# An RWKV block on one core: last tile's output stored in three parts from two queues, flag of inexact weights formed four steps sooner

## Chip, cores and metric

The kernel runs on one core of one Trainium2 chip. The metric is the device time of one execution in microseconds (us); the number to predict is the median of unprofiled runs. The engines are named as the profile names them: PE is TensorE's matmuls and PEld its weight loads, DVE is VectorE, ACT is ScalarE, POOL is GpSimd and SP is SyncE.

## The reference

Input `x` is (2, 4096, 256) in float32. An RWKV layer with a layer norm ahead of it, then a gated feed-forward layer with a layer norm ahead of it:

```python
x = x + attn(layernorm(x))      # W_k, W_v, W_r, a scan over time, W_o
x = x + ffn(layernorm(x))

def ffn(x):                     # D_IN 256, D_HID 1024; w1, w2, h1, h2, w3 hold -1, 0 or 1
    h = silu(tlin(x, w1_w, w1_s)) * tlin(x, w2_w, w2_s)
    h = gelu(tlin(h, h1_w, h1_s))
    h = gelu(tlin(h, h2_w, h2_s))
    return tlin(h, w3_w, w3_s)
```

`tlin(x, w, s)` is `x @ w.T * s`.

## The kernel before

Features lie on the 128 partitions and time on the free axis. Time is cut into 16 tiles of 512 steps (2 batches of 8). A tile of `x` is `[128, 2, 512]` float32, 512 KB: two halves of the 256 features, numbered h=0 and h=1. The result is summed into the same tile, `x_sb` (called `x1` in `ffn`), and stored from it.

`split_block` does the work. Its feed-forward weights are held rounded to a format in which the matmul takes one pass (float32r), and each activation is split into a rounded part `hi` and a rest `lo`, so that every product takes two matmuls, L172 for `hi` and L173 for `lo`. This gives the wanted result only if the rounding left the weights unchanged. So the kernel compares the given weights with the rounded ones while it runs (`compare`, on tiles 1 to 15), and sums the counts of differences at the end: `total` on DVE (L629), the matmul `everywhere` with a constant matrix, which brings the sum to all partitions (L631), and `inexact`, an integer 0 or 1, on DVE (L633). Every engine then reads `inexact` into a register (L60) and branches (L61): if it is 1, `general_block` computes everything again in plain float32. With the weights of the reference it is 0, and all engines branch over that block. The closing barrier of the program carries the line of the launch, L908.

For tile i, `ffn(i)` is a generator that yields 26 times. Steps 0 to 7 make the gated products (`pa`, `pb`); steps 8 to 15 are the first hidden layer and steps 16 to 23 the second, both with eight groups of 16 matmuls into `ph`, each followed by two ACT instructions (L580, L582) and a DVE subtraction that makes `lo` (L583). The second layer's weights come from HBM in eight blocks, `h2_sb`, that SP loads (L576). Steps 24 and 25 are the output product for h=0 and h=1: 16 matmuls into `po`, and one DVE instruction that adds the result to `x_sb` (L595). After that POOL issues one DMA for the tile (L599). Between the steps the loop takes steps of the next tiles' attention and layer norm, but there are none left during the last tile.

The order on each engine is that of a scheduler that works by priority of the program's order, unless an `issue_after` ties an instruction down. In the program before, the order at the end is: on PE the last `po` group, then `everywhere`, then the register load; on DVE the two L595, then `inexact`; on SP the last `h2_sb` load, then the register load; on POOL the last store, then the register load. `total` is placed far earlier, at 1431.7 us.

Of the kernel before, what the change touches and what calls it, by code (L numbers as in the profile page):

```python
# [8 lines left out]
F32 = mybir.dt.float32  # L9
F32R = mybir.dt.float32r  # L10
AF = mybir.ActivationFunctionType
ALU = mybir.AluOpType

P = 128
# [3 lines left out]
NH = HID // P  # L18
# [47 lines left out]
def split_block(ctx, tc, flags, x, vecs, w_attn, w1, w2, h1, h2, w3, out):  # L66


    nc = tc.nc
    tensor, vector, scalar = nc.tensor, nc.vector, nc.scalar  # L70
# [9 lines left out]
    ps_attn = ctx.enter_context(tc.tile_pool(name="ps_attn", bufs=3, space=bass.MemoryType.PSUM))  # L80
# [3 lines left out]
    tiles = [(b, n) for b in range(B) for n in range(NT)]  # L84

    def hbm(t, b, n):
        return t[b, :, n * TS : (n + 1) * TS].rearrange("(h p) t -> p h t", p=P)

    whole = slice(0, TS)
    halves = [slice(k * TS // 2, (k + 1) * TS // 2) for k in range(2)]  # L90
# [11 lines left out]
    for m, queue in enumerate((nc.scalar, nc.sync, nc.sync)):  # L102
# [6 lines left out]
        out=ident, in_=ident, compare_op=ALU.not_equal, fill=1.0, base=0, pattern=[[-1, P]], channel_multiplier=1  # L109
# [16 lines left out]
    mean_w = const.tile([P, P], F32, name="mean_w")  # L126
# [15 lines left out]
    pieces = []  # L142
# [4 lines left out]
    rounded = const.tile([P, len(pieces) + NH * (NH * P // PIECE)], F32, name="rounded")  # L147
    found = iter(range(rounded.shape[1]))

    def compare(kept, given, shape):  # L150
        raw = tmp.tile(shape, F32, tag="full", name="raw")
        nc.gpsimd.dma_start(out=raw, in_=given)
        j = next(found)
        vector.scalar_tensor_tensor(
            raw, raw, 1.0, kept.bitcast(F32), ALU.mult, ALU.not_equal, accum_out=rounded[:, j : j + 1]
        )

    def col(base, j):
        return vec[:, base + j : base + j + 1]
# [7 lines left out]
    def split_product(psum, weights, src):  # L167

        n = len(src)
        for c in range(n):  # L170
            hi, lo = src[c]
            tensor.matmul(psum, weights(c), hi, start=c == 0, stop=False)  # L172
            tensor.matmul(psum, weights(c), lo, start=False, stop=c == n - 1)  # L173
# [3 lines left out]
    def split(hi, lo, full):  # L177

        marks["rounded"] = scalar.activation(hi, full, AF.Copy)  # L179
        marks["rest"] = vector.tensor_tensor(lo, full, hi.bitcast(F32), ALU.subtract)  # L180
# [92 lines left out]
    def normalise(i):  # L273

        x_sb = loaded.pop(i)
        if i + 1 < len(tiles):
            loaded[i + 1] = load_x(i + 1)
        xn = []

        def new_xn():  # L280

            xn.append(one.tile([P, ND, TS + 1], F32, tag="xn", name="xn"))
            if tiles[i][1] == 0:
                vector.memset(xn[0][:, :, 0:1], 0.0)
            else:
                vector.tensor_copy(xn[0][:, :, 0:1], prev)
            return xn[0][:, :, 1:]

        yield from layernorm(x_sb, new_xn, "rstd1", pause=i == 1)
        vector.tensor_copy(prev, xn[0][:, :, TS:])  # L290
        normal[i] = (x_sb, xn[0])
# [107 lines left out]
    def first_tile(second):  # L399
# [59 lines left out]
        attn, ffn = (ps_attn, "pa"), (ps_ffn, "pf")  # L459
        keys = [[(project(0, 0, attn, p), p) for p in halves], [(project(0, 1, attn), whole)]]  # L460
        v = [project(1, h, ffn) for h in range(ND)]
        r = [project(2, h, ffn) for h in range(ND)]

        def differences(h):
# [47 lines left out]
        for p in halves:  # L512
            add(y[:, 1, p], so[1][0][:, p], r[1][:, p], ALU.mult)
        banks = [
            [pool.tile([P, TS // 2], F32, tag=tag, name="ps_o") for pool, tag in kinds]
            for kinds in ((attn, attn), (attn, ffn))
        ]
        for c in range(ND):
# [28 lines left out]
    def hidden():  # L547
        return (
            hid.tile([P, TS], F32R, tag="hi", name="hi"),
            hid.tile([P, TS], F32R, tag="lo", name="lo"),  # L550
        )

    def ffn(i, x1, x2):

        checks = pieces[2 * (i - 1) : 2 * i] if i > 0 else []
        ha = []
        for f in range(NH):
            fs = slice(f * P, (f + 1) * P)
            pa = ps_ffn.tile([P, TS], F32, tag="pf", name="pa")
            split_product(pa, lambda c: w1_sb[:, c, fs], x2)  # L560
            pb = ps_ffn.tile([P, TS], F32, tag="pf", name="pb")
            split_product(pb, lambda c: w2_sb[:, c, fs], x2)
            full = tmp.tile([P, TS], F32, tag="full", name="gated")
            scalar.activation(full, pa, AF.Silu, scale=col(S1, f))  # L564
            vector.scalar_tensor_tensor(full, pb, col(S2, f), full, ALU.mult, ALU.mult)  # L565
            hi, lo = hidden()
            split(hi, lo, full)
            ha.append((hi, lo))
            yield
        for layer, scales in enumerate((SH1, SH2)):  # L570
            src, ha = ha, []
            for f in range(NH):
                fs = slice(f * P, (f + 1) * P)
                if layer == 1:
                    block = stream.tile([P, NH, P], F32R, tag="h2", name="h2_sb")
                    nc.sync.dma_start(out=block.bitcast(F32), in_=h2_hbm[f].bitcast(F32))  # L576
                ps = ps_ffn.tile([P, TS], F32, tag="pf", name="ph")
                split_product(ps, lambda c: block[:, c, :] if layer else h1_sb[:, c, fs], src)
                hi, lo = hidden()
                scalar.activation(hi, ps, AF.Gelu, scale=col(scales, f))  # L580
                full = tmp.tile([P, TS], F32, tag="full", name="full")
                scalar.activation(full, ps, AF.Gelu, scale=col(scales, f))  # L582
                vector.tensor_tensor(lo, full, hi.bitcast(F32), ALU.subtract)  # L583
                ha.append((hi, lo))
                if layer == 0 and f % 4 == 0 and checks:
                    compare(*checks.pop(), [P, PIECE])
                if layer == 1 and i == f + 1:
                    n = PIECE // P
                    for c in range(0, NH, n):
                        compare(block[:, c : c + n, :], h2[:, c : c + n, fs], [P, n, P])  # L590
                yield
        for h in range(ND):
            ps = ps_ffn.tile([P, TS], F32, tag="pf", name="po")
            split_product(ps, lambda c: w3_sb[:, c, h * P : (h + 1) * P], ha)
            vector.scalar_tensor_tensor(  # L595
                x1[:, h, :], ps, col(S3, h), x1[:, h, :], ALU.mult, ALU.add
            )
            yield
        nc.gpsimd.dma_start(out=hbm(out, *tiles[i]), in_=x1)  # L599

    def run(steps):
        for _ in steps:
            pass

    normal, got = {}, {}
    second = normalise(1)
    first_tile(second)
    for i in range(len(tiles)):
        ahead = attention(i + 1) if i + 1 < len(tiles) else iter(())
        further = normalise(i + 2) if i + 2 < len(tiles) else iter(())  # L610
        for step, _ in enumerate(ffn(i, *got.pop(i))):
            if i == 0:
                if step in (1, NH - 1):
                    with tc.issue_after(marks["rounded"].ins), tc.issue_after(marks["rest"].ins):
                        next(second)
                elif step == NH:
                    run(second)

            for _ in range(0 if step < NH else 4 if step == NH + (i == 0) else 1):
                next(ahead, None)  # L620
            if step > 2 * NH - 6 and step % 2 == 0:
                next(further, None)
        run(ahead)
        run(further)
    assert len(pieces) <= 2 * (len(tiles) - 1)


    total = flags.tile([P, 1], F32, name="total")
    vector.tensor_reduce(total, rounded, mybir.AxisListType.X, ALU.add)  # L629
    everywhere = ps_attn.tile([P, 1], F32, tag="pa", name="everywhere")  # L630
    tensor.matmul(everywhere, mean_w, total, start=True, stop=True)  # L631
    inexact = flags.tile([P, 1], mybir.dt.int32, name="inexact")
    vector.tensor_scalar(inexact, everywhere, 0.0, None, ALU.is_gt)  # L633
    return inexact[0:1, 0:1]


# [275 lines left out]
```

## Time and profile before

| | us |
|---|---|
| median of 3 runs without a profile | 1572.11 (1571.52 to 1572.32) |
| the profiled execution, whole | 1574.68 |
| its span, first to last instruction | 1572.90 |
| PE busy | 1559.1 |
| DVE busy | 1102.0 |
| ACT busy | 1034.4 |
| POOL busy | 62.0 |
| last matmul of the output product starts | 1562.62 |
| last addition to `x_sb` starts (0.75 long) | 1563.06 |
| last store issued | 1564.11 |

The span counts from the first instruction to the last; what lies around it belongs to the launch and is not resolved. The granted TensorE clock was 0.997 of full speed over the span. Durations of matmuls are modelled, so a busy PE is not PE at its peak. A page shows the instruction groups with the most busy time; the register loads, branches, semaphore waits and drains of the program's end don't count as busy and are found by asking for their source line.

### The profile page before, as it was taken

What the parts mean: (1) busy time and instruction counts of PE and PEld (TensorE: products, weight loads), DVE (VectorE), ACT (ScalarE), POOL (GpSimd) and SP (SyncE); (2) the same over time, 40 slices, a digit from 0 to 9 for tenths busy, and PEclk for the clock granted to TensorE, in tenths of its full rate; (3) what the DMA queues carried; (4) which work ended last, traced back from release to release, by engine and by line L of the source; (5) the groups of instructions that cost most, each with busy time, mean ns of one, the idle gap of its engine ahead of it and who ended that gap; (6) DMA issues with size and microseconds to landing.
All of it is one profiled execution on the core that took longest, in us unless ns stands there. A gap on an engine that the chain in (4) does not pass through costs nothing.

```text
span 1572.9 us, 16652 instructions
## 1 busy us (share of the span) xinstructions
PE 1559.1 (99%) x6319; PEld 1185.9 (75%) x6319; DVE 1102.0 (70%) x1763; ACT 1034.4 (66%) x1394; POOL 62.0 (4%) x99
## 2 busy tenths in 40 slices
PE   9999999999999999999999999999999999999997
PEld 5768777777777778777787777877777787777886
DVE  6788686776768767786786867767687676865521
ACT  5676767667577585776767666675776857756542
POOL 3000000000000000000000000000000000000000
PEclk9999999999999999999999999999999999999999
DMA  9102031220402204021130311203112030211202
GB/s 360 42 32 103 14 121 34 73 88 9 130 30 75 79 20 134 14 90 65 34 121 14 107 48 47 94 14 108 41 64 78 21 108 27 80 48 34 94 14 69
DMA packets 36598, 109.16 MB, mean 69 GB/s; under 512 B 3680, under 2 KB 12384, under 8 KB 36000
## 3 DMA queue, kind: packets, MB, share of 16 engines
q1 hardware_dynamic: 19136, 67.93, 13.0%
q0 software_dynamic: 16960, 39.59, 8.1%
q8 instruction: 51, 0.84, 0.2%
q10 hardware_dynamic: 416, 0.52, 0.1%
q14 instruction: 35, 0.29, 0.1%
HBM read 99.64 MB, written 12.58 MB: 71 GB/s over the span
## 4 chain that ended last, share of the span: by engine, by line
PE 80%; issue 15%; DVE 2%; ACT 1%; DMA 1%; POOL 0%; POOLq 0%; DVEq 0%
PE ph L172 24%; PE ph L173 24%; PE pb L172 3%; PE pa L172 3%; PE pb L173 3%; PE pa L173 3%; PE po L173 3%; PE po L172 3%; PE ps_k L165 3%; PE ps_r L165 3%; PE ps_v L165 3%; PE ps_o L165 3%; PE mean L201 1%; DVE scale L342 0%; PE var L201 0%
## 5 line engine op out<-in xcount | busy, mean ns | idle before, releaser
L172 PE MATMUL ph<-hi,h_sb 128*128 128x512 f32 x2048 | 813.8, 397 | 0.0
L173 PE MATMUL ph<-lo,h_sb 128*128 128x512 f32 x2048 | 801.4, 391 | 0.0
L172 PEld LDWEIGHTS ph<-hi,h_sb 128*128 128x128 f32 x2048 | 384.9, 188 | 92.7 <-issue 11.7
L173 PEld LDWEIGHTS ph<-lo,h_sb 128*128 128x128 f32 x2048 | 385.0, 188 | 88.6 <-issue 8.4
L583 DVE TENSOR_TENSOR lo<-full,hi 128x512 fp32r<-128x512 f32 x256 | 175.4, 686 | 174.7 <-ACT full L582 173.6
L580 ACT ACTIVATE hi<-ph,vec 128x512 fp32r<-128x512 f32 x256 | 175.7, 686 | 183.3 <-PE ph L173 181.9
L582 ACT ACTIVATE full<-ph,vec 128x512 f32<-128x512 f32 x256 | 174.2, 681 | 0.9 <-DVE lo L583 0.8
L565 DVE SCALAR_TENSOR_TENSOR gated<-pb,vec,gated 128x512 f32<-128x512 f32 x128 | 95.5, 748 | 58.2 <-PE pb L173 31.0
L580 ACT ACT_TABLE_LOAD x102 | 130.9, 1283 | 1.8
L564 ACT ACTIVATE gated<-pa,vec 128x512 f32<-128x512 f32 x128 | 86.5, 684 | 59.7 <-PE pa L173 56.5
L220 DVE RECIPROCAL rstd<-rstd 128x512 f32<-128x512 f32 x30 | 100.4, 3346 | 5.3 <-ACT rstd L218 5.3
L172 PE MATMUL pb<-x_hi,w_sb 128*128 128x512 f32 x256 | 102.1, 399 | 0.6 <-DVE gated L565 0.6
L172 PE MATMUL pa<-x_hi,w_sb 128*128 128x512 f32 x256 | 102.0, 398 | 0.1
L173 PE MATMUL pb<-x_lo,w_sb 128*128 128x512 f32 x256 | 100.7, 393 | 0.0
L173 PE MATMUL pa<-x_lo,w_sb 128*128 128x512 f32 x256 | 100.6, 393 | 0.0
L173 PE MATMUL po<-lo,w_sb 128*128 128x512 f32 x256 | 100.3, 392 | 0.0
L172 PE MATMUL po<-hi,w_sb 128*128 128x512 f32 x256 | 100.1, 392 | 0.0
L179 ACT ACTIVATE hi<-gated 128x512 fp32r<-128x512 f32 x128 | 80.6, 630 | 27.9 <-DVE gated L565 26.5
L180 DVE TENSOR_TENSOR lo<-gated,hi 128x512 fp32r<-128x512 f32 x128 | 87.7, 686 | 5.3 <-ACT hi L179 0.7
L248 DVE TENSOR_TENSOR_SCAN lm<-vec,lm,ps_k 128x512 f32<-128x512 f32 x30 | 38.3, 1278 | 42.9 <-PE ps_k L165 42.8
L303 DVE SCALAR_TENSOR_TENSOR mx<-xn,vec,mx 128x512 f32<-128x512 f32 x90 | 66.4, 744 | 0.3
L595 DVE SCALAR_TENSOR_TENSOR x_sb<-po,vec,x_sb 128x512 f32<-128x512 f32 x32 | 24.0, 751 | 58.9 <-PE po L173 58.9
(144 smaller groups left out, 1815.8 us busy)
## 6 DMA issues: line engine op xcount, KB each, us to landing
h_sb<-h_hbm SPq DMA_DIRECT2D x128, 512.0 KB, 3.3
out<-x_sb POOLq DMA_DIRECT2D x16, 512.0 KB, 3.1
raw<-in_h POOLq DMA_DIRECT2D x32, 256.0 KB, 3.1
x_sb<-in_x POOLq DMA_DIRECT2D x15, 512.0 KB, 4.1
h_sb<-in_h POOLq DMA_DIRECT2D x1, 4096.0 KB, 20.6
h_hbm<-in_h POOLq DMA_DIRECT2D x8, 512.0 KB, 22.9
w_sb<-in_w POOLq DMA_DIRECT2D x3, 1024.0 KB, 11.4
raw<-in_w POOLq DMA_DIRECT2D x12, 256.0 KB, 2.8
```

Source lines behind the costliest of these rows:

```text
L165: tensor.matmul(psum, weights(c), src[c], start=c == 0, stop=c == n - 1)
L172: tensor.matmul(psum, weights(c), hi, start=c == 0, stop=False)
L173: tensor.matmul(psum, weights(c), lo, start=False, stop=c == n - 1)
L179: marks["rounded"] = scalar.activation(hi, full, AF.Copy)
L180: marks["rest"] = vector.tensor_tensor(lo, full, hi.bitcast(F32), ALU.subtract)
L220: vector.reciprocal(rstd, rstd)
L303: vector.scalar_tensor_tensor(mx[:, h, :], xn[:, h, 1:], vec[:, j : j + 1], mx[:, h, :], ALU.mult, ALU.add)
L564: scalar.activation(full, pa, AF.Silu, scale=col(S1, f))
L565: vector.scalar_tensor_tensor(full, pb, col(S2, f), full, ALU.mult, ALU.mult)
L580: scalar.activation(hi, ps, AF.Gelu, scale=col(scales, f))
L582: scalar.activation(full, ps, AF.Gelu, scale=col(scales, f))
L583: vector.tensor_tensor(lo, full, hi.bitcast(F32), ALU.subtract)
```

## The change

In the last tile each half of the features is stored as soon as it is added. Half h=0 is one DMA of 256 KB from SP's queue. Half h=1 is two DMAs of 128 KB, its first 256 time steps from SP's queue and the other 256 from ACT's. POOL stores only the tiles 0 to 14, as before. The three operations that form the flag move into a function that is called after step 22 of the last tile, that is, ahead of the last `ph` group and of the output product; the assertion ahead of the loop is a check at build time.

```diff
@@ ffn @@
             vector.scalar_tensor_tensor(
                 x1[:, h, :], ps, col(S3, h), x1[:, h, :], ALU.mult, ALU.add
             )
-            yield
-        nc.gpsimd.dma_start(out=hbm(out, *tiles[i]), in_=x1)
+
+            if i == len(tiles) - 1:
+                for queue, p in ((nc.sync, halves[0]), (nc.scalar, halves[1])) if h else ((nc.sync, whole),):
+                    queue.dma_start(out=hbm(out, *tiles[i])[:, h, p], in_=x1[:, h, p])
+            yield
+        if i < len(tiles) - 1:
+            nc.gpsimd.dma_start(out=hbm(out, *tiles[i]), in_=x1)
@@ split_block @@
+    def any_inexact():
+
+        total = flags.tile([P, 1], F32, name="total")
+        vector.tensor_reduce(total, rounded, mybir.AxisListType.X, ALU.add)
+        everywhere = ps_attn.tile([P, 1], F32, tag="pa", name="everywhere")
+        tensor.matmul(everywhere, mean_w, total, start=True, stop=True)
+        inexact = flags.tile([P, 1], mybir.dt.int32, name="inexact")
+        vector.tensor_scalar(inexact, everywhere, 0.0, None, ALU.is_gt)
+        return inexact
+
+    assert len(pieces) <= 2 * (len(tiles) - 1)
...
             if step > 2 * NH - 6 and step % 2 == 0:
                 next(further, None)
+            if i == len(tiles) - 1 and step == 3 * NH - 2:
+                inexact = any_inexact()
         run(ahead)
         run(further)
-    assert len(pieces) <= 2 * (len(tiles) - 1)
-
-
-    total = flags.tile([P, 1], F32, name="total")
-    vector.tensor_reduce(total, rounded, mybir.AxisListType.X, ALU.add)
-    everywhere = ps_attn.tile([P, 1], F32, tag="pa", name="everywhere")
-    tensor.matmul(everywhere, mean_w, total, start=True, stop=True)
-    inexact = flags.tile([P, 1], mybir.dt.int32, name="inexact")
-    vector.tensor_scalar(inexact, everywhere, 0.0, None, ALU.is_gt)
     return inexact[0:1, 0:1]
```

The scheduled order of the changed program on the queues that it touches: on PE `everywhere` stands ahead of the last `ph` group. On DVE `inexact` stands behind the sixth `lo` of the second layer (1549.78 in the profile before) and ahead of the seventh (1553.40). On SP the register load stands behind the last `h2_sb` load, then come the two stores, then the branch. On ACT the store stands behind the last L582, then the register load, then the branch. On POOL the register load follows the store of tile 14.

## The prediction

> **What bounds the kernel now.** I read the busy times of the page first, then the timeline of the last tile, then the instruction groups by source line of the program's end, and the waits of SyncE's queue last.
>
> ```profile
> PE 1559.1 (99%) x6319; PEld 1185.9 (75%) x6319; DVE 1102.0 (70%) x1763; ACT 1034.4 (66%) x1394; POOL 62.0 (4%) x99
> ```
>
> TensorE is busy for 99% of the span, back to back, so nothing earlier is worth anything unless it shortens the matmul stream. The change doesn't: the number of matmuls stays, and one is only moved. What it can reach is the stretch in which TensorE has already stopped. The timeline of that stretch:
>
> ```profile
> 1562.62 0.40 PE L173 MATMUL po<-lo,w_sb 128*128 128x512 f32 x1
> ...
> 1562.86 0.28 PE L631 MATMUL everywhere<-total,mean_w 128*128 128x1 f32 x2
> 1563.06 0.75 DVE L595 SCALAR_TENSOR_TENSOR x_sb<-po,vec,x_sb 128x512 f32<-128x512 f32 x1 [2.91 <-PE po L173]
> 1563.73 0.15 DVE L633 TENSOR_SCALAR inexact<-everywhere 128x1 int32<-128x1 f32 x1
> 1564.11 0.73 POOL L599 DMA_DIRECT2D out<-x_sb  x1 [79.86 <-DVE inexact L633]
> ```
>
> The last useful matmul ends at 1563.02, the last output half is in SBUF at 1563.81, and the span ends at 1572.9. Nearly 10 us hold one 512 KB store and the program's end. POOL's row blames the flag (L633), but by the program's order its store waits for x_sb (L595, done 1563.81) and starts 0.30 later. The groups of L60 (every engine reads the flag into a register), L61 (every engine branches over the general block) and L908 (the closing barrier) show who comes last (durations are smallest/median/largest in ns, then the first and last start in us; a q after the engine's name is its queue):
>
> ```profile
> L60 ACTq TENSOR_LOAD <-inexact x1: 469/469/469, 1563.9 to 1563.9; - x1
> L60 DVEq TENSOR_LOAD <-inexact x1: 542/542/542, 1563.9 to 1563.9; - x1
> ...
> L61 ACTq COMPARE_BRANCH  x1: 50/50/50, 1564.4 to 1564.4; - x1
> L61 PEldq COMPARE_BRANCH  x1: 4422/4422/4422, 1564.5 to 1564.5; - x1
> ...
> L61 ACTq EVENT_SEMAPHORE  x1: 17/17/17, 1567.0 to 1567.0; - x1
> L61 DVEq EVENT_SEMAPHORE  x1: 21/21/21, 1567.7 to 1567.7; - x1
> L61 PEldq EVENT_SEMAPHORE  x1: 51/51/51, 1569.0 to 1569.0; - x1
> ...
> L908 POOLq DRAIN  x3: 51/113/7234, 1564.8 to 1572.6; - x3
> L908 SPq DRAIN  x3: 7/7/7, 1570.2 to 1572.3; - x3
> ```
>
> No engine may branch before the flag exists at 1563.9, and after the branch ACT needs 2.5 us to its next instruction (1564.44 to 1566.95), DVE 3.1 (1564.53 to 1567.68), PE 4.4; in that time the trace has fetches on the instruction queues. SyncE waits for the store before it joins the barrier:
>
> ```profile
> SPq L908 <- DMA out<-x_sb: 3.7, 1, 3.7
> DMA to landing us min/median/max: 3.0/3.1/5.5
> ```
>
> The second line is of the stores of L599: 3.1 us usually, 5.5 for this last one, whose final ring reports at 1569.64, 2.6 us after most of the others, while instruction fetches of 8 and 16 KB run. SyncE then works through ten more waits and arrives at 1570.27. The very last is POOL: its drain, begun at 1564.82 behind its store, lasts 7.23 us, to 1572.06. From there the barrier takes 0.84 to the end (1572.90). So the order of arrival is ACT 1567.0, DVE 1567.8, PE 1569.1, SP 1570.3, POOL 1572.1.
>
> **The change, part by part.** All sums are against the profiled execution: 1574.68 us, of which 1572.90 are span and 1.78 lie around it. The unprofiled median is 1572.11, 2.57 less; I carry a difference over to it unscaled.
>
> *The flag four steps sooner.* In the changed program's order the matmul `everywhere` stands ahead of the last `ph` group (about 1551.9), `inexact` between two `lo` subtractions; the reduction `total` stays where it ran (1431.7). The matmul has two passes. A row for its price: the 128x1 passes of the first tile (`var`, L342) start 0.11 apart. Two make 0.22 us that now stand inside the stream instead of after it; bounds 0.1 (one pass hidden) and 0.5 (two exposed weight loads of 0.19 and a refill). I take **+0.2**. On DVE `inexact` (0.15) runs at about 1552.5; behind it in the queue stands a `lo` that can't start before 1553.4, so it costs nothing as long as `everywhere` isn't late by 0.9.
>
> *Everybody's register load.* SP and POOL read the flag near 1552.5 and are through. On SP the load now stands before the two stores, behind the last `h2` load (1544.84), so nothing is held up. PE's queue runs ahead of its array: its wait for the last h2 block is recorded at 1548.14, the matmul that needs the block runs near 1551.9. The last `lo` that PE must wait for is ready at 1557.7, so its load and branch should be dispatched near 1560 and its 4.42 us of refill end by 1565, under the closing matmuls: PE's arrival falls from 1569.1 to about 1563.8.
>
> *The store.* POOL loses its last L599 store; with no transfer of its own since 1483.5 its drain should start near 1553, and even at 7.2 us it ends by 1561. SP gets h=0 (256 KB, issued near 1560.4, done by about 1563 under the last eight matmul pairs) and half of h=1; ACT gets the other half. h=1 is ready at 1563.81 + 0.2 = 1564.0. A steady SP issue lasts 0.32 and its first packet runs 0.95 after its start, against 0.73 and 1.31 for POOL's store; POOL's late start of 0.3 goes too (ACT and SP reacted to `inexact` within 0.04). 2 x 128 KB are half of a store of 3.1: I take 2.3 to landing, 1566.4; bounds 2.0 and 5.5 (this store's own row). Then SP's waits at 0.06 each: SP arrives at about **1567.1**.
>
> *What is late next.* ACT has its store ahead of its flag load: 1564.0 + 0.5 issue (its two DMAs at the start took 0.48 and 0.51) + 0.5 load + 0.1 branch + 2.5 refill = **1567.6**. DVE's load stands right behind its last L595: it starts between 1563.3 (its queue runs on) and 1564.05, so 0.54 + 0.08 + 3.15 later DVE arrives at 1567.1 to **1567.9**. The last arrival is near 1567.75; with 0.84 of barrier the span ends at 1568.6, **4.3 us sooner**: 1572.11 - 4.3 = 1567.8.
>
> *Two rules weighed.* The trace's branches took 2.5 to 4.4 us until the next instruction. The Trainium skill, "Advanced Engine Details and Errata", Control Flow Timing, puts a compare-and-branch at about 108 ns. By that figure ACT and DVE would arrive at 1565.2 and SP's landing alone would set the end: 1567.1 + 0.84, a gain of 5.0. "Runtime: NRT & Kernel Launch", Instruction fetch mechanics, says that a taken branch out of the prefetched window must fetch its target first; the rows side with that, so I keep 2.5 to 3.15. And against splitting h=1 over two queues: "DMA: Bandwidth & Descriptors", Issuing engines are not separate DMA queues, says that a second issuing engine saves only the sequencer's issue time. Here that is 0.32 on SP, bought with 0.5 on ACT, ahead of a branch that I find critical. With both halves on SP ACT would be out of the way; the rule makes this edit worth nothing or -0.1, the rest stays.
>
> **The rivals.**
>
> *A, as above, 62%:* 1567.8, own range 1566.8 to 1568.8. For it: every term has a row.
>
> *B, the drain is shorter without the profiler, 15%.* The profiled run is 2.57 us above the median; if that excess sits in POOL's 7.23 us, the unprofiled end was set by SP at 1570.3, and the change brings 1570.3 - 1567.75 = 2.5: **1569.6**. Against it: 2.57 us may lie anywhere in 1572, and SP's own straggler could shrink likewise.
>
> *C, PE does not run ahead across a register load, 11%* (the flag is sooner, yet frees nobody). Then PE loads at 1563.25, 0.55 + 4.42 + 0.15: arrival 1568.4, end 1569.2, gain 3.7: **1568.4**. Against it: the waits recorded 3.8 us ahead of their matmuls.
>
> *D, the store straggles again, 8%.* ACT's and DVE's fetches fall on 1565 to 1567, the very time of the last 256 KB; landing 5.5 after issue gives 1569.6, SP 1570.2, gain 1.0: **1571.1**. For it: the same happened before; against: a ring now carries 16 KB in this stretch instead of 32, and PE's 16 KB fetch has moved away.
>
> *E, the drain moves with the store, 4%: slower.* If L908's drain takes 7.2 us on any engine whose DMA is recent, ACT's, begun at 1567.6, lasts to 1574.8: 2.8 later than POOL's now, **1574.9**; it is slower as soon as the drain on ACT passes 4.4. Against: SP's drain lasted 7 ns only 0.6 us after the store it waited for had landed, but that store was POOL's; SP's own last DMA was long done, which is why this can't be excluded.
>
> **How the numbers follow.** About 0.2% (3.1 us) is what a measurement of this kernel can tell from no change; that is below 1569.0. Faster by more: nearly all of A (0.60), most of C (0.09), a little of B and of what lies beyond A's lower end (0.06): 0.75. Within: the rest of A and C, most of B, D: 0.21. Slower: E, of which only the worse part passes 0.2%, and an unforeseen cost of the inserted matmul: 0.04. The range 1566.4 to 1569.9 takes in A, B, C and the landing bound of 2.0; D and E are left out with the edges of A and B.
>
> **What would show it.** In the changed profile: `everywhere` near 1552 and the last `po` matmul 0.1 to 0.5 later than 1562.62; the flag loads of SP and POOL near 1552.5, of PE near 1560; the branch of PE begun before the last matmul; POOL's long drain ended before 1562; the landing of the last two stores at 1566 to 1567; ACT or DVE last into the barrier, between 1567.1 and 1568. It is wrong if the 7 us drain is still the last row, if PE's branch again starts after its last matmul, or if SP still waits for a landing after 1569.

## The result, and the profile after

The changed kernel takes 1569.61 us (median of 22 runs, 1568.36 to 1572.23) against 1572.84 for the kernel before, measured beside it (22 runs, 1571.52 to 1574.98): ratio 0.998, 95% interval 0.9974 to 0.9986. That is 3.2 us less (2.2 to 4.1). In the profiled execution (1570.85 us, span 1569.1) the work before the program's end is the same:

```profile
PE 1559.1 (99%) x6319; PEld 1184.3 (75%) x6319; DVE 1102.3 (70%) x1763; ACT 1035.0 (66%) x1394; POOL 60.0 (4%) x98
```

The timeline at the place where the flag is now formed (start and duration in us):

```profile
1551.56 0.39 PE L173 MATMUL ph<-lo,h_sb 128*128 128x512 f32 x1
1551.56 0.41 PEld L615 LDWEIGHTS everywhere<-total,mean_w 128*128 128x128 f32 x2
1551.78 0.28 PE L615 MATMUL everywhere<-total,mean_w 128*128 128x1 f32 x2
...
1551.92 0.47 PE L172 MATMUL ph<-hi,h_sb 128*128 128x512 f32 x1
...
1552.10 0.16 DVE L617 TENSOR_SCALAR inexact<-everywhere 128x1 int32<-128x1 f32 x1 [1.75 <-PE everywhere L615]
...
1552.23 0.39 PE L173 MATMUL ph<-lo,h_sb 128*128 128x512 f32 x1
```

From the matmul before the insertion to the second one behind it are 0.67 us, where two steps of the stream take 2 x 0.227 = 0.45 (0.227 is the mean step between matmul starts from 1530 to 1562 in the profile before): the insertion costs the stream 0.22 us. Then the end, on the timeline of all engines:

```profile
1562.77 0.40 PE L173 MATMUL po<-lo,w_sb 128*128 128x512 f32 x1
1563.21 0.75 DVE L595 SCALAR_TENSOR_TENSOR x_sb<-po,vec,x_sb 128x512 f32<-128x512 f32 x1 [2.92 <-PE po L173]
1563.98 0.34 SPq L601 DMA_DIRECT2D out<-x_sb  x1
1563.99 0.38 ACTq L601 DMA_DIRECT2D out<-x_sb  x1
```

No POOL row is left. The groups of L60, L61 and the closing barrier (L917 in the changed file), durations in ns, then first and last start in us:

```profile
L60 PEldq TENSOR_LOAD <-inexact x1: 489/489/489, 1558.9 to 1558.9; - x1
L60 DVEq TENSOR_LOAD <-inexact x1: 541/541/541, 1563.2 to 1563.2; - x1
L60 ACTq TENSOR_LOAD <-inexact x1: 609/609/609, 1564.4 to 1564.4; - x1
...
L61 SPq EVENT_SEMAPHORE  x8: 17/17/17, 1566.9 to 1567.4; - x8
...
L61 PEldq COMPARE_BRANCH  x1: 3322/3322/3322, 1559.5 to 1559.5; - x1
...
L61 ACTq COMPARE_BRANCH  x1: 54/54/54, 1565.1 to 1565.1; - x1
...
L61 ACTq EVENT_SEMAPHORE  x1: 17/17/17, 1567.8 to 1567.8; - x1
...
L917 POOLq DRAIN  x3: 51/107/4715, 1553.0 to 1568.8; - x3
L917 SPq DRAIN  x3: 7/7/7, 1568.2 to 1568.5; - x3
```

The order of arrival is now POOL 1557.7 (its drain of 4.7 begins at 1553.0), PE 1563.4, DVE 1567.2, ACT 1567.9 and SP last, 1568.26. From there 0.81 to the end. SP waits for its own stores. The group of L601 gives the time from issue to landing (the last report that the data has been written) of the three:

```profile
DMA to landing us min/median/max: 2.5/2.9/3.1
```

and the waits of SP's queue (total, number, longest) the time that it stood at the line of the branch, with nothing but its own landing to wait for:

```profile
SPq L61 <- SPq L61: 2.5, 1, 2.5
```

The trace has 16 reports of completion for each store, and what reports is called a ring here. The store from SP is issued at 1563.98; 15 of its 16 rings report by 1565.79, the last at 1566.84. Only then does SP begin its list of waits, in which it checks one semaphore after another, those of the transfers and those of the other engines: 1566.86 to 1568.26.

### The profile page after: what moved, and what is told of

Its sections match the earlier page's. It is cut to its first block, busy times and chain, and to the rows that moved or that the text cites. A ratio compares the mean times of both kernels' runs of the same rounds, so it can differ in the third digit from the quotient of the medians.

```text
span 1569.1 us, 16653 instructions
## 1 busy us (share of the span) xinstructions
PE 1559.1 (99%) x6319; PEld 1184.3 (75%) x6319; DVE 1102.3 (70%) x1763; ACT 1035.0 (66%) x1394; POOL 60.0 (4%) x98
## 4 chain that ended last, share of the span: by engine, by line
PE 97%; DVE 2%; DMA 1%; ACT 0%; issue 0%; DVEq 0%; POOLq 0%
PE ph L172 30%; PE ph L173 30%; PE po L173 4%; PE po L172 4%; PE pb L172 4%; PE pa L172 4%; PE pb L173 4%; PE pa L173 4%; PE ps_k L165 3%; PE ps_r L165 3%; PE ps_v L165 3%; PE ps_o L165 3%; PE mean L201 1%; PE var L201 1%; DVE scale L342 0%; DMA out<-x_sb 0%
## 5 line engine op out<-in xcount | busy, mean ns | idle before, releaser
L582 ACT ACTIVATE full<-ph,vec 128x512 f32<-128x512 f32 x256 | 174.5, 682 | 0.9 <-DVE lo L583 0.8
```

## The experiments

The moment when the matmul stream ends wanders from execution to execution: the start of the last `po` matmul, P, lay between 1560.84 and 1563.01 in the fourteen profiles. Of that, up to 1.95 us are in the first tile (first `pa` matmul at 43.19 to 45.14), and tiles 8 to 11 take from 382.5 to 383.4 us. Neither belongs to the change. So I read the end of the program from P to the end of the span:

| kernel | P | span end | end from P |
|---|---|---|---|
| before (three looks) | 1562.62, 1560.84, 1561.37 | 1572.90, 1570.83, 1571.44 | 10.27, 10.00, 10.07 |
| changed (two) | 1562.77, 1561.74 | 1569.07, 1568.07 | 6.30, 6.33 |
| flag sooner alone (two) | 1561.29, 1561.79 | 1569.37, 1569.86 | 8.08, 8.07 |
| store alone | 1561.60 | 1569.16 | 7.56 |
| h=1 as one DMA from SP (two) | 1563.01, 1562.47 | 1568.71, 1568.43 | 5.70, 5.96 |
| whole tile as one DMA from SP | 1561.01 | 1567.42 | 6.41 |
| last addition in halves | 1562.06 | 1567.93 | 5.87 |
| changed, no branch | 1561.24 | 1565.68 | 4.44 |
| before, no branch | 1562.61 | 1570.41 | 7.81 |

Where the flag is formed sooner, 0.22 us have to be added for the insertion ahead of P. Looks at one kernel differ by up to 0.27 in this end, so smaller differences between kernels with one or two looks say little. The theory at the start was T: POOL's drain, 7.2 us behind its own store, ended the program, and taking the store from POOL brings the gain.

**The changed kernel again** (no edit). 

> The changed kernel once more, to have it beside the others on one chip. Theory T (the end was set by POOL's drain behind its own store; now by SyncE's landing and its list of waits): the profile repeats its rows within 0.5 us: last arrival SyncE at 1568.0 to 1568.5, POOL's drain 4 to 5 us and over by 1558, span about 1569; median 3.2 us under the kernel before. Rival R (the gain is a chance placement of the store's slowest ring): arrival of SyncE anywhere between 1567 and 1570, gain 1 to 4.

1569.10 against 1572.81, ratio 0.9979 (0.9970 to 0.9988). SP arrived last at 1567.25, which is ahead of the time that T named and inside R's window, but P was 1.03 us earlier than in the first profile. From P the rows repeat: POOL's drain 4.715 us, SP last at P + 5.51 against P + 5.49, its slowest ring again 1.1 behind the others. That is T and not the chance placement of R.

**The flag alone.** The loop of the stores is taken out again:

```diff
-            if i == len(tiles) - 1:
-                for queue, p in ((nc.sync, halves[0]), (nc.scalar, halves[1])) if h else ((nc.sync, whole),):
-                    queue.dma_start(out=hbm(out, *tiles[i])[:, h, p], in_=x1[:, h, p])
             yield
-        if i < len(tiles) - 1:
-            nc.gpsimd.dma_start(out=hbm(out, *tiles[i]), in_=x1)
+        nc.gpsimd.dma_start(out=hbm(out, *tiles[i]), in_=x1)
```

> The flag four steps sooner alone; POOL stores the last tile whole, as before. T: POOL's store is issued near 1564.25 and its drain starts near 1565; with a recent store of its own it takes about 7.2, so POOL arrives near 1572.2, the span ends near 1573.0 and nothing is gained (0 to +0.3), although PE has branched early and the store's slowest ring lands at about 1567.5 instead of 1569.6, since PE's 16 KB fetch is out of its way. Rival D (the drain ends a fixed 2.4 after the last landing): POOL arrives near 1570, a gain of 2 to 3. Rival F (the early flag is what brings the gain): a gain of about 3.2, span near 1569.

1572.13, ratio 0.9993 (0.9985 to 1.0001). The closing barrier (L913 here):

```profile
L913 POOLq DRAIN  x3: 51/112/5034, 1563.5 to 1569.1; - x3
L913 SPq DRAIN  x3: 7/7/7, 1566.7 to 1568.8; - x3
...
L913 PEldq DRAIN  x2: 8/8/8, 1561.9 to 1568.9; - x2
```

T's drain of 7.2 is refuted: it is 5.03 here, POOL still comes last (1568.5), and the slowest ring lands 3.3 after the issue (1566.11) instead of 5.5. POOL's drain ends 2.414 after that landing. In the kernel before it ended 1572.057 - 1569.643 = 2.414 after it. So D takes the place of T's fixed length: the drain lasts until 2.41 after the landing of POOL's last store, and at least 4.7. By P the flag alone is worth 10.11 - 8.08 - 0.22 = 1.8 us, a little less than the 2 to 3 of D; the medians (0.7, interval -0.2 to 2.4) can't tell that from nothing.

**A second look at it.** 

> The flag sooner alone, a second look: its timed runs fall in two groups, 1570.3 to 1571.1 and 1572.1 to 1572.7, and the first profile is of the lower. D: in the upper group a ring of POOL's store is held up by DVE's fetch or PE's second one and lands 1 to 1.5 later, and the drain with it (2.41 behind). Rival: the landing is as before and the matmul stream ended later.

This profile took 1571.64, between the two groups, so none of the upper group was seen. The drain again ends 2.415 after the landing and the end is P + 8.07; the 0.5 us between the two looks lie in P alone. That speaks for the rival, the stream's own wandering, but does not settle it for the upper group. In both looks the last ring reports only 0.27 behind the others: the 8 KB instruction fetch that follows DVE's branch (from P + 2.1, 0.57 long) is over before the first packet of POOL's store (P + 2.79).

**The store alone.**

```diff
-            if i == len(tiles) - 1 and step == 3 * NH - 2:
-                inexact = any_inexact()
         run(ahead)
         run(further)
+    inexact = any_inexact()
```

> The store in three parts from SyncE and ScalarE alone; the flag is formed behind the last matmul, as before. T: POOL reads the flag at 1564.1 and starts its drain near 1564.8; without a recent store it takes 4.7 as in the changed kernel, so POOL arrives near 1569.5 and PE, whose refill starts at 1564.5, near 1569.0; span near 1570.2, a gain of 2.5 to 2.9, not the whole. Rival F (the early flag brings the gain): PE at 1569 and SyncE's landing straggling to 1569, gain under 1. Rival S (the store alone brings all): span 1569, gain 3.2 or more, since the 0.15 us of the moved matmul is saved.

1571.49, ratio 0.9990 (0.9981 to 0.9998). The barrier (L916 here):

```profile
L916 POOLq DRAIN  x3: 51/107/4715, 1563.6 to 1568.9; - x3
L916 SPq DRAIN  x3: 7/7/7, 1567.9 to 1568.6; - x3
...
L916 PEldq DRAIN  x2: 8/8/8, 1567.9 to 1568.7; - x2
```

The three stores (L601):

```profile
DMA to landing us min/median/max: 1.8/2.0/2.1
```

By P it is worth 10.11 - 7.56 = 2.55, as T said, where F had under 1 and S 3.2 or more; by the medians 1.3 (0.3 to 3.0). POOL, which has stored nothing since tile 14, still pays 4.7 from the moment at which it may branch, and comes last at 1568.32; PE, whose refill (the time from its branch to its next instruction) starts at 1563.5, arrives at 1567.87, and SP, whose list waits for PE's arrival, at 1567.96. So it takes the early flag to get both out of the way. The row of the stores is the other finding: without the early flag the three stores land 1.8 to 2.1 after their issue, with it 2.5 to 3.1. Here the fetches begin at 1564.41, when the last packets of the store have all but passed (1564.48); in the changed kernel, where the packets run from 1564.82, two fetches of 8 KB begin amid them, at 1564.91 and 1565.52. By their places they are DVE's and SP's: each begins 1.1 behind that engine's branch (P + 1.07 and P + 1.61), and where SP branches at P + 2.80 (the last addition in halves, below) the second one comes at P + 3.93. ACT's, at 1566.26, meets only the end of the slowest ring. The early flag, which lets SP and DVE branch while the store is in flight, costs the landing about 1 us.

**No branch.** From the changed kernel:

```diff
-    count = nc.values_load(inexact, min_val=0, max_val=1)
-    with tc.If(count > 0):
-        with ExitStack() as inner:
-            general_block(inner, tc, x, vecs, w_attn, w1, w2, h1, h2, w3, out)
```

> The changed kernel without the register loads, the branch and the general block behind it: the flag is formed and read by nobody. Times are from the start of the last po matmul (P), because its own place moves by a us from run to run. T (the slowest ring of the last store is held up by ACT's and DVE's instruction fetches): landing at P + 3.0 to 3.3 with no ring later than 0.3 after the others, SyncE's list 1.3 behind it, span end at P + 5.0 to 5.5 instead of 6.3. Rival R (the ring is slow by itself): one ring still reports about 1 us after the rest, span end at P + 6.0 to 6.4.

1567.15, ratio 0.9964 (0.9950 to 0.9978); end at P + 4.44, below what T expected. The three stores (L597 here):

```profile
DMA to landing us min/median/max: 1.9/2.0/2.1
```

All 16 rings of the last SP store report within 0.23 us, and there is no instruction fetch in the trace beyond 1555. With the store alone, where the fetches came too late to meet the packets, the rings were as close (0.23). So the fetches are what holds up one ring, and R falls. The rest of the surprise is SP's list: without the branch it has about half as many waits (11 semaphore rows from its first wait to the end instead of 22) and takes 0.55 us behind the landing instead of 1.40. One row of the barrier (L913) bears on rival E:

```profile
L913 ACTq DRAIN  x2: 8/80/152, 1562.9 to 1565.2; - x2
```

ACT's drain began at 1562.87, right behind the issue of its own store, and was over after 0.15 us, while that store landed at 1564.52: a drain on ACT does not wait for ACT's store.

**The kernel before, no branch** (the same edit). 

> The kernel before without the register loads, the branch and the general block. Two forms of the drain stand against each other. D (POOL's drain lasts 4.715, or until 2.41 after the landing of POOL's last store, whichever is later; both numbers from the runs so far): landing without fetches at P + 4.4 to 4.6, drain over at P + 6.8 to 7.1, span end at P + 7.6 to 8.0 instead of 10.3. T as first stated (7.2 whenever POOL has just stored): drain over at P + 9.4, span end at P + 10.2.

1570.77, ratio 0.9989 (0.9980 to 0.9998). The barrier (L904 here):

```profile
L904 POOLq DRAIN  x3: 51/102/5558, 1564.1 to 1570.1; - x3
```

With no fetch the last store, issued at 1564.09, lands at 1567.16, all rings within 0.2; the drain ends at 1569.63, 2.46 behind. D said P + 6.8 to 7.1, measured P + 7.0; T's fixed 7.2 is out. The landing comes 2.3 sooner than in the kernel before (P + 4.55 against a mean of P + 6.86), and so does the end (7.81 against 10.11). In the kernel before, then, 2.3 of the 10.1 us at the end came with the branch, from fetches on the store's ring, and they were paid in full because POOL's drain followed the landing.

**The kernel before, twice more.** 

> The kernel before once more, to see whether its end (10.3 from the start of the last po matmul, P, to the end of the span) is typical. By D (POOL's drain ends 2.41 after the last ring of its store) the end is the landing + 3.3: 10.3 if the slowest ring again lands at P + 7.0; 7.8 if no ring is held up. The medians, 3.2 to 3.7 above the changed kernel's, whose end is P + 6.3, say that it lies at P + 9.5 to 10.3 in most runs.

 

> As before_2: end at P + 9.5 to 10.3 if the held-up ring is the rule; D's difference of 2.4 between the last landing and the drain's end within 0.1 in any case.

The stores (L599) of the second, the last of them the longest:

```profile
DMA to landing us min/median/max: 3.0/3.1/5.3
```

and its barrier (L908):

```profile
L908 POOLq DRAIN  x3: 51/112/7027, 1563.6 to 1571.2; - x3
```

Both again hold up one ring to 5.3 behind the issue; the drains are 6.954 and 7.027 long and end 2.415 and 2.416 after the landing. Ends of P + 10.0 and 10.1: the held-up ring is the rule in this kernel. The profiled executions took 1572.61 and 1573.22, so the first one's 1574.68 lay high by chance.

**One DMA from SP for the whole tile.** The loop of the stores goes, as with the flag alone, and the last store changes its queue (only the new line is shown):

```diff
+        (nc.gpsimd if i < len(tiles) - 1 else nc.sync).dma_start(out=hbm(out, *tiles[i]), in_=x1)
```

> The flag sooner, the last tile stored whole (512 KB) by one DMA from SyncE. T (what counts is that POOL doesn't store; splitting saves the transfer of 256 KB): landing 0.6 to 0.9 later than with two parts from SyncE (there P + 4.0), SyncE's list 0.9 behind it, span end at P + 6.3 to 6.7, that is 0 to 0.4 above the changed kernel's. Rival P (the parts are what brings the gain): span end at P + 8 or later.

1570.49, ratio 0.9981 (0.9972 to 0.9990), end at P + 6.41, against 6.32 of the changed kernel: the three parts bring 0.1 us, which is within the spread of two looks. The barrier (L913):

```profile
L913 POOLq DRAIN  x3: 51/107/4715, 1551.3 to 1567.1; - x3
L913 SPq DRAIN  x3: 7/7/7, 1566.5 to 1566.8; - x3
```

The store lands at P + 4.64, only 0.2 ahead of POOL's in the kernel with the flag alone (P + 4.82). The two kernels differ only in the engine that stores, and end at P + 6.41 and P + 8.07: POOL's drain no longer follows the landing. What counts is that POOL isn't the one that stores.

**h=1 as one DMA from SP.**

```diff
-                for queue, p in ((nc.sync, halves[0]), (nc.scalar, halves[1])) if h else ((nc.sync, whole),):
+                for queue, p in ((nc.sync, whole),):
```

> The changed kernel with both parts of h=1 as one DMA from SyncE; ScalarE stores nothing. T: ScalarE's load and branch run near 1557.5 and it is at the barrier by about 1561; only VectorE's fetch still meets the store. SyncE's last landing at 1566.2 to 1566.9, its last wait 0.6 to 1.35 later: arrival 1567.3 to 1568.0, span near 1568.4, 0.3 to 1.2 us under the changed kernel. Rival W (a second queue is worth its place): landing 0.3 us or more later than with two queues and no less straggling, span equal to the changed kernel's or up to 0.5 longer.

 

> h=1 as one DMA from SyncE, a second look: its end was P + 5.7 against P + 6.3 of the changed kernel, a difference too small for the medians. T: again P + 5.6 to 5.9, SyncE last, 0.9 behind its landing.

1569.08, ratio 0.9976 (0.9966 to 0.9985): the medians see no difference to the changed kernel. The stores (L601) of the first look:

```profile
DMA to landing us min/median/max: 2.5/2.7/2.8
```

ACT is at the barrier at 1559.4; the last ring lands at P + 4.0 and P + 4.3, no later than with two queues, and SP's remaining waits take 0.9 instead of 1.40, since this store's semaphore is the eighth of the list and not the first. The end is 0.4 to 0.6 shorter in both looks; the second (5.96) was just above what T named. The order of the list is not all of it: the last row of SP's list waits for ACT's arrival, reported at P + 5.09 in the changed kernel and at P - 3.7 here. Behind that report SP could not have been through before about P + 5.2, against P + 5.49 measured, so the order explains at most 0.3 and the rest needs ACT out of the way. Nor is ACT's own fetch needed for the late ring, which stays 0.6 behind the next one without it. W, that the second queue is worth its place, has nothing for it.

**The last addition in halves.** h=0 from POOL, h=1 as two additions of 256 columns, each stored from SP (the new lines, in place of the addition and the loop of the stores):

```diff
+            for p in halves if last_tile and h else (whole,):
+                vector.scalar_tensor_tensor(
+                    x1[:, h, p], ps[:, p], col(S3, h), x1[:, h, p], ALU.mult, ALU.add
+                )
+                if last_tile:
+                    (nc.sync if h else nc.gpsimd).dma_start(out=hbm(out, *tiles[i])[:, h, p], in_=x1[:, h, p])
```

> A try at a faster one: flag sooner; h=0 stored by POOL; the last addition to h=1 made in two halves of 256 columns, each stored from SyncE as soon as it is there; ScalarE stores nothing. By D POOL is done by P + 3.2, under the rest. The last store is 128 KB, issued at P + 1.25: landing at P + 3.1 to 3.3, or up to P + 4.0 if DVE's fetch holds a ring; list 0.9; span end at P + 4.9 to 5.7, against 6.3 of the changed kernel and 5.7 of two parts from SyncE. Rival V (the second instruction and its own issue cost what the smaller store saves): P + 5.7 to 6.0.

1569.70, ratio 0.9977 (0.9967 to 0.9987), end at P + 5.87, inside what V named. The stores (L601):

```profile
L601 SPq DMA_DIRECT2D out<-x_sb x2: 341/876/1410, 1563.0 to 1563.4; - x2
```

The second issue, at once behind the first, holds SP for 1.41 us instead of 0.34 and eats what the smaller store saves. The runs don't show why: four loads that SP issues one behind the other at the program's start take 0.42 to 0.46 us each, and the second half of the addition was done before this issue began. POOL was done at P + 3.34, where D had 3.2.

No version that keeps the branch is shown to beat the changed kernel's time; the one with h=1 in one DMA from SP has the shorter end in its profiles, at equal medians.

## Why the prediction was right, point by point

- *The number.* 1569.61 lies in the stated range (1566.4 to 1569.9), but above A's own (1566.8 to 1568.8), and on the figure of rival B (1569.6). That it hits B's figure is chance: B's mechanism has nothing for it in the runs (below), while A's shows in the rows. A's figure was too low by a base that lay 0.7 higher and a gain that was 0.7 to 1.1 smaller.
- *What bounds the end.* The main step held: POOL's drain was the last arrival before (1572.06), and it is gone with the store. What I took as a length of 7.2 is 4.7 at least, or 2.41 behind the landing (2.414 to 2.416 in five profiles, 2.46 in the one without branch). For the changed kernel that makes no difference: 4.7 from 1553.0 is over by 1557.7.
- *The matmul moved into the stream:* 0.2 taken, 0.22 measured. `inexact` runs at 1552.1, more than a us ahead of the `lo` behind it (1553.28 in the trace), and costs nothing, as said.
- *PE ahead of its array:* the register load was expected near 1560 and came at 1558.9; the branch took 3.32, under the closing matmuls, against 4.42 before. Rival C falls.
- *The landing:* 1566.4 taken, 1566.84 (SP) and 1567.06 (ACT) measured. The landing was 0.4 late. The term that was mis-sized most is SP's way to the barrier: 0.7 taken (it was 0.6 behind the landing by the rows of before), and it is 1.40, because SP's list checks this store's semaphore first and all others behind it; before, the late semaphore stood in the middle. Together SP came at 1568.26 instead of 1567.1, and SP, not ACT or DVE, is the last. The fetches on the store's ring I had put into rival D as a straggler of 5.5; they cost 1.0 instead. D's sum was also wrong: SP at 1570.2 and 0.84 of barrier end the span at 1571.0, a gain of 1.9 and not of 1.0, so that D stood for 1570.2 and not for 1571.1.
- *ACT and DVE:* 1567.6 and at most 1567.9 taken; 1567.92 and 1567.24 measured. ACT's refill took 2.75 and its load 0.61, each a little over the rows of before.
- *The two rules.* The 108 ns that the Trainium skill, "Advanced Engine Details and Errata", Control Flow Timing, gives for a compare-and-branch have no counterpart here but the instruction's own duration, 45 to 72 ns on ACT, DVE, SP and POOL; from ACT's branch to its next row are 2.7 us. The other rule, of "DMA: Bandwidth & Descriptors", Issuing engines are not separate DMA queues, that a second issuing engine saves only issue time, agrees with the runs: one DMA from SP lands no later than two from two queues. ACT's store in front of its branch cost more than the 0 to 0.1 that I had weighed for it: without it the end is 0.4 to 0.6 shorter.
- *The sum.* 4.3 forecast. By P: 10.11 - 6.32 - 0.22 = 3.6; by the medians 3.2 (2.2 to 4.1). Of the missing 0.7, 0.5 is SP's later arrival against the 1567.75 that I had put last, and 0.2 the first profile of before, whose end of 10.27 was 0.16 above the mean of three. The time of 1567.8 was forecast from a median of 3 runs, 1572.11; over 22 runs the kernel before has 1572.84, so 0.7 of the 1.8 between 1567.8 and 1569.61 is the base, not the change.
- *Rival B* rested on a profiled run 2.57 above the median. The other two profiled runs of the same kernel (1572.61 and 1573.22) lie at the median of 1572.84, with drains of 7.0, so nothing is left of its ground; what the drain takes in an unprofiled run no trace can show. *Rival E* falls: ACT's and SP's drains took 7 to 8 ns, and in the kernel without the branch ACT's was over while its own store was still in flight.

## What to carry to other kernels

Ask who arrives last at the end of the program, engine by engine, before shortening any part of it: here neither half of the change brought the whole by itself (1.8 and 2.55 us, together 3.6), since each left POOL's drain as the last arrival, behind its store or behind its late branch. In this kernel the closing store was 1.7 us cheaper from SP, whose drain is short, than from POOL (P + 6.41 against P + 8.07), and a branch that came early enough had PE's refill under the last matmuls. And an effect of 0.2% in a kernel whose matmul stream wanders by 2 us is read more surely from a fixed point near the end of the trace than from the medians of a dozen runs, as long as what the change costs ahead of that point (0.22 us here) is added.

## What the runs showed of the hardware that was not expected

- POOL's drain at the program's end: 4.715 us, the same to the ns, in six profiles in which POOL's last store was over 65 us back; and an end 2.414 to 2.416 after the landing of the store where that was recent (2.46 without the branch). Where POOL stored only h=0 (the last addition in halves) the drain took 4.80, a little over what both numbers give. What it does in that time no run shows.
- Instruction fetches of 8 and 16 KB that run amid a store's packets hold up some of its rings, and one of them most: the last reports 0.5 to 1.1 us behind the bulk where one or two fetches met the packets, 2.2 to 2.5 in the kernel before, where several of 8 KB and PE's of 16 KB did, and 0.3 to 0.4 where a fetch was just over before the first packet. Where none came near, all 16 report within 0.23.
- PE takes a branch with its refill while its array still works through 3.3 us of dispatched matmuls: its branch began at 1559.50 and the last matmul at 1562.77.
- In one profile a second store issued from SP directly behind the first took 1.41 us to issue instead of 0.34, although loads issued one behind the other at the start took 0.42 to 0.46. The cause stays open.
